# Cross-attention on one core: where SyncE's queue puts the rows of x and the tokens' values

## The chip, the core and the metric

The kernel runs on one core of a Trainium2 chip. A core has TensorE (PE: matmuls, with weight loads shown as PEld), VectorE (DVE), ScalarE (ACT), GpSimd (POOL) and SyncE (SP); each runs its own instruction stream, and they wait for one another by semaphores. Transfers between HBM and the on-chip memory are issued from SyncE's, ScalarE's or GpSimd's stream. The metric is the device time of one execution in microseconds (us).

## What is computed

`x` is 16 batches of 100 rows of 640; `ctx` is 16 batches of 722 rows of 384, of which the last 4 rows are "tokens" and the first 718 the context. There are 8 heads of 80. All is float32.

```python
query, keyt, valt = x @ Wq, enc @ Wk, enc @ Wv
hs = _mha(query, keyt, valt)                     # 100 queries over 718 keys
ca_q1 = einsum('btc,th->bch', ca, Wq_ca)[:, indices, :]
ca_hs1 = _mha(ca_q1, x, x)                       # attention over the rows of x
ca_q2 = ca_hs1 @ Wq
ca_hs2 = _mha(ca_q2, ca @ Wk_ca, ca @ Wv_ca)     # 100 queries over 4 tokens
out = (hs + ca_hs2) @ Wout + b_out + x
```

## The kernel before

A loop runs over the 16 batches `b`; the order of the instructions on each engine is the order in which the loop writes them out. In a batch PE first makes the scores (`s_ps`, L716) in three parts, with a small product `z_ps` (L934) of the token branch. VectorE takes their running maximum; the last of these maxima is called `seen` (`larger(2)`, L1380). Then PE makes values of this batch (`v_ps...`, L434, class `Values`) in turns with keys of the next (`k_ps...`, L465, class `Keys`), while VectorE and ScalarE spread the maximum, subtract it and take exponentials. At the end of the batch PE multiplies the exponentials with the values (`a_ps`, L1585: the "product with V"), makes a small product `y_ps` (L880) for a later batch, and the next batch's scores follow at once.

GpSimd does the token branch. `scores1` (L905, L912) waits for `seen`; `values2` (L1002, L1009) multiplies the values of the four tokens, spread over 100 partitions, with probabilities and adds them up. Those values lie in tiles `vb` of 250 KB: two buffers, filled for tokens 0 and 1 by `Second.load`, and for tokens 2 and 3 by SyncE out of `values2`, when the product that read the buffer before is done. `Second.load` issues its two transfers from GpSimd's stream, in the batch before the one that uses them (`second.load()`), except for batches 0 and 1. GpSimd also makes the sums `enc` (L500) that the keys and values of the next batch need, from `enc` and `rest`, which SyncE loads.

The output rows are cut into groups of 128 (`OC`); five times two of these groups are projected as a pair (`PAIRS`, `project_pair`, `o_ps` L1160, with sums on GpSimd, L1141). `Last.load` fetches the rows of `x` (`xn`, 320 KB a group) from SyncE's stream, and GpSimd adds the bias to them (L1042), so that the projection can be added on top.

SyncE's stream is worked off in order, and a transfer that waits for a semaphore holds up those behind it. In a batch it holds, in this order: rows of x where there are any, values of tokens 2 and 3, inputs of the batch after next (`xT`, `ca`, `enc`, and the small `mb`), and `rest`, which waits for PE's last key product. The rows of x stand next behind `rest` of the batch before, without a wait of their own. `wait_for(instruction, other)` makes one instruction wait for another one.

Of the kernel before, what the change touches and what calls it, by code (L numbers as in the profile page):

```python
# [126 lines left out]
def kernel(  # L127
# [18 lines left out]
    nc = tc.nc  # L146
# [131 lines left out]
    for g in range(2):  # L278
        for c in range(CC):
            nc.scalar.dma_start(  # L280
                out=wv_sb[:, 2 * c + g],
                in_=wv[c * P : (c + 1) * P, g * (H // 2) : (g + 1) * (H // 2)],
# [42 lines left out]
    for h, c, r, s, k in PIECES:  # L325
        nc.gpsimd.dma_start(
            out=m2[s : s + k, c, h - HEADS[c][0], :T],
            in_=wqcat[h * D + r : h * D + r + k, :],
# [4 lines left out]
    for c in range(HC):  # L333
        first = c * P - HEADS[c][0] * D
        nc.gpsimd.affine_select(
            out=hmask[:, c], in_=hmask[:, c], compare_op=ALU.is_ge, fill=0.0,
# [3 lines left out]
            out=hmask[:, c], in_=hmask[:, c], compare_op=ALU.is_ge, fill=0.0,  # L340
# [439 lines left out]
    def wait_for(ins, other):  # L780

        tc.add_manual_dep(
            ins.ins,
            other.ins.name,
            mybir.DependencyInfo(
                mybir.DependencyClass.Sync, mybir.DependencyReason.DATA
            ),
            reason="apart",
        )
# [69 lines left out]
    class Second:  # L859
# [87 lines left out]
            )  # L947
            self.z = z

        def load(self):  # L950
            self.vb = [self.piece(nc.gpsimd, t) for t in range(2)]

        def piece(self, engine, t):
            b = self.b
            vb = vb_tile(f"vb_{b}_{t}")
            engine.dma_start(
                out=vb[:S], in_=va_d[b * T + t].unsqueeze(0).to_broadcast([S, H])
            )
            return vb

        def scores2(self, engine=nc.vector):
# [61 lines left out]
    class Last:  # L1023
# [4 lines left out]
            self.split = b == B - 1  # L1028
            self.t_ps = None

        def load(self):

            self.xn = {}
            for r, (lo, n) in enumerate(OC):
                if self.b != O_AFTER[r]:
                    continue
                xn = self.xn[r] = spare[1] if r == len(OC) - 1 else xn_tile(f"xn_{r}")
                rows = x.rearrange("b s n -> (b s) n")[lo : lo + n]
                for at, cols in self.parts(n):
                    to = xn[at : at + n, : cols.stop - cols.start]  # L1040
                    nc.sync.dma_start(out=to, in_=rows[:, cols])
                    nc.gpsimd.tensor_tensor(to, to, bias[at : at + n, cols], ALU.add)  # L1042

        def parts(self, n):
# [201 lines left out]
    for n, heads in enumerate(HEADS):  # L1246
        cols = len(heads) * B * T
# [26 lines left out]
    second = Second(0, xT, ca_0)  # L1274
# [71 lines left out]
    for b in range(B):  # L1346
        p = b // 2
        e_in, now = enc, second
# [35 lines left out]

        if b == 0:
            enc_sums(enc)
            now.load()
            now.softmax1()
        st.append(scores(b, 0, tiles))
        if b == 0:  # L1390
# [15 lines left out]
        if b == 0:  # L1406
            second.scores1()
            m_next = load_m(b + 2)
            kk.go(3)
            top.go(3)  # L1410
            first_values(3, e_in, (act, act), get=bank)
            top.go(1)
            kk.go(2)
            now.scores2()
            now.exponentials2()
            first_values(0, e_in, (act, act), (0,), bank)
            top.go()
            kk.go(3)
            first_values(0, e_in, (act, act), (1,), bank)
            now.softmax3()  # L1420
            kk.go(2)
            subtract(0)
            exponential(0)
            kk.go(2)
            subtract(1)
            kk.go(3)
            exponential(1)
            second_next, enc_next = loads()
            less = subtract(2)
            exponential(2)  # L1430
            last_keys(b + 1, enc)
            enc_next = load_rest(b + 2, enc_next)
            keys(m_next)
            now.values2(less)
            enc_sums(enc_next)
            second.softmax1(4)
        elif b + 1 < B:
            vv = Values(b, e_in)

            def both(n):  # L1440
                vv.go(n)
                kk.go(n)

            forms = [wout_sb[:, 2 * i : 2 * i + 2, k * (H // 2) : (k + 1) * (H // 2)]
                     for i in range(2) for k in range(2)]
            if b == 2:
                for o, left, right in (
                    (forms[1], forms[1], forms[0]),
                    (wout2[:, 0], forms[3], forms[1]),
                    (wout2[:, 1], forms[2], wout2[:, 0]),  # L1450
                ):
                    nc.gpsimd.tensor_tensor(o, left, right, ALU.subtract)
            elif last.b - 1 in PAIRS:
                nc.gpsimd.tensor_tensor(wout2[:, 0], wout2[:, 0], forms[0], ALU.add)
            second.scores1(seen, range(T - 1))
            top.go(3)
            kk.go(3)
            vv.go(3)
            now.scores2(nc.gpsimd)
            second.scores1(None, range(T - 1, T))  # L1460
            if b == 1:
                now.load()
            last.load()
            top.go(1)
            if b > 1:
                last.place()
            now.exponentials2()
            both(2)
            both(2)
            top.go()  # L1470
            both(1)
            now.softmax3()
            if b == 1:
                nc.gpsimd.tensor_tensor(last.hs[:S], last.hs[:S], last.hs2, ALU.add)
            if last.b in PAIRS:
                last.sums()
            parted = b % 2 and b > 1 and last.b not in PAIRS
            now.values2(None, range(T - 1 if parted else T))
            vv.go(2)
            kk.go(1)  # L1480
            subtract(0)
            exponential(0)
            vv.go(1)
            subtract(1)
            vv.go(1)
            kk.go(2)
            exponential(1)
            vv.go(1)
            kk.go(2)
            both(1)  # L1490
            both(1)
            if b == 1:
                for f in list(wv_there):
                    nc.scalar.copy(wv_sb[:, W_AT[f]], wv_there.pop(f))
            mixed = None
            if b % 2 and b > 1:
                second_next, enc_next = loads()
                mixed = Queries(p + 1, xT_at[0], enc_next[0])
            if parted:
                mixed.sums()  # L1500
                now.values2(None, range(T - 1, T))
            else:
                second.load()
            if b == 1:
                nc.gpsimd.dma_start(out=bias, in_=bout[0].partition_broadcast(P))
            if not mixed:
                second_next, enc_next = loads()
            if b + 2 < B:
                m_next = load_m(b + 2)
            subtract(2)  # L1510
            exponential(2)
            last_keys(b + 1, enc)
            if b + 2 < B:
                enc_next = load_rest(b + 2, enc_next)
            if b == 1:
                last.transpose()
            if last.b in PAIRS:
                second.softmax1(3)
                last.project_pair()
                if last.b == max(PAIRS):  # L1520
                    nc.sync.dma_start(
                        out=forms[1],
                        in_=wout[: 2 * P, H // 2 :].rearrange("(c p) n -> p c n", p=P),
                    )
            second.softmax1(3 if parted else 8)
        else:
            room = enc_tile("spare").rearrange("p f k -> p (f k)")
            spare.extend(room[:, i * H : (i + 1) * H] for i in range(2))
            last.transpose()
            vv = Values(b, e_in)  # L1530
            last.load()
            mine.load()
            top.go(3)
            vv.go(3)
            last.project_few(len(OC) - 2)
            now.scores2(nc.gpsimd)
            now.exponentials2()
            top.go(1)
            vv.go(2)
            top.go()  # L1540
            vv.go(3)
            now.softmax3()
            now.values2()
            vv.go(2)
            subtract(0)
            exponential(0)
            vv.go(5)
            for i in (1, 2):
                subtract(i)
                exponential(i)  # L1550
            last.project()
        if b % 2 and b + 1 < B:
            xT, tiles = xT_at[0], queries_tiles(p + 1)
            if not mixed:
                for n in range(HC):
                    queries(p + 1, xT, tiles, n)
            elif parted:
                mixed.make(tiles, second.softmax1)
                second.load()
            else:  # L1560
                keys(m_next)
                mixed.sums()
                mixed.make(tiles, second.softmax1)
# [109 lines left out]
```

## Time and profile before

| | us |
|---|---|
| median of 3 runs | 922.90 |
| lowest and highest run | 922.18, 924.91 |
| profiled execution | 922.65 |
| its span, first to last instruction | 920.94 |
| PE busy in it | 911.9 |

The profile gives the busy time of each engine, who waited for whom and for how long, a timeline, the instructions and the DMA load of any stretch of time, and the chain of work that ended last. "Issue" as the releaser of a wait stands for idle time in which the engine waited for nothing that the profile shows. Times in the timeline count from the start of the span.

### The profile page before, as it was taken

The page shows a single profiled execution, that of the slowest core. Times are in us where ns is not written, and L with a number is a line of the kernel's source. Part 1 is how long each engine was busy: PE and PEld are TensorE (multiplying, and loading weights), DVE is VectorE, ACT ScalarE, POOL GpSimd, SP SyncE. Part 2 cuts the span into 40 slices and gives each one's busy share as a digit, 9 for nine tenths or more (in the row PEclk, how much of TensorE's full clock was granted, in tenths as well). Part 3 has the DMA queues.
Part 4 walks back from the last instruction along what each step waited for, and adds up shares of the span by engine and source line. Part 5 has one row for each costly group of instructions (what it writes and reads, how often), then busy time and mean ns, then how long its engine had stood idle before and what let it go on. Part 6 is the DMA issues. An engine that isn't in the chain of part 4 may idle for free.

```text
span 920.9 us, 27684 instructions
## 1 busy us (share of the span) xinstructions
PE 911.9 (99%) x11974; PEld 766.2 (83%) x11974; DVE 692.5 (75%) x1116; ACT 434.4 (47%) x836; POOL 723.6 (79%) x689
## 2 busy tenths in 40 slices
PE   9999999999999999999999999999999999999998
PEld 6988879787797979888798887988879888797966
DVE  3469895988649887795967869689784898748883
ACT  2234543737427373552737436264741737426341
POOL 5849999788977879697896969958798687976623
PEclk9999999999999999999999999999999999999999
DMA  8722013050300404031030410205030050310201
GB/s 270 269 77 78 25 49 95 1 156 2 104 32 11 119 1 134 3 97 60 24 111 3 117 40 30 77 2 155 3 101 33 2 157 1 104 46 3 81 23 38
DMA packets 49681, 62.94 MB, mean 68 GB/s; under 512 B 14072, under 2 KB 38200, under 8 KB 49560
## 3 DMA queue, kind: packets, MB, share of 16 engines
q1 hardware_dynamic: 45512, 51.49, 18.3%
q0 software_dynamic: 3024, 8.53, 3.0%
q8 instruction: 94, 1.54, 0.7%
q10 hardware_dynamic: 1024, 1.15, 0.4%
q14 instruction: 27, 0.22, 0.1%
HBM read 55.59 MB, written 5.57 MB: 66 GB/s over the span
## 4 chain that ended last, share of the span: by engine, by line
PE 97%; DVE 1%; DMA 0%; POOL 0%; issue 0%; ACT 0%; SPq 0%; ACTq 0%; POOLq 0%
PE s_ps L716 12%; PE a_ps L1585 11%; PE v_psA L434 11%; PE v_psB L434 9%; PE k_psA L465 8%; PE kT_ps L666 8%; PE k_psB L465 7%; PE o_ps L1160 5%; PE v_psC L434 4%; PE k_psC L465 3%; PE v_ps L375 2%; PE q_ps L593 2%; PE q_ps L535 2%; PE v_psD L434 2%; PE v_psE L434 2%; PE q_psA L593 1%
## 5 line engine op out<-in xcount | busy, mean ns | idle before, releaser
L905 POOL TENSOR_TENSOR e<-ca,g 100x800 f32<-100x800 f32 x64 | 99.4, 1564 | 91.8 <-ACT kT L407 64.3
L500 POOL TENSOR_TENSOR enc<-enc 128x240 f32<-128x240 f32 x135 | 106.6, 800 | 18.2 <-DMA enc<-in_enct 11.1
L1368 DVE TENSOR_TENSOR st<-st,over 120x1600 f32<-120x1600 f32 x48 | 113.8, 2373 | 0.0
L1585 PEld LDWEIGHTS a_ps<-vs,st 120*36 120x36 f32 (+3 forms) x3072 | 109.4, 124 | 3.9 <-issue 3.1
L1585 PE MATMUL a_ps<-vs,st 120*36 120x81 f32 (+3 forms) x3072 | 111.9, 233 | 0.3 <-ACT st L1376 0.3
L434 PE MATMUL v_psA<-wv_sb,enc 128*120 128x320 f32 x352 | 109.3, 433 | 0.0
L1009 POOL TENSOR_TENSOR hs<-hs,hs 100x640 f32<-100x640 f32 x48 | 96.3, 2007 | 3.8
L912 POOL TENSOR_TENSOR e<-e,e 100x800 f32<-100x800 f32 x48 | 92.1, 1919 | 3.8
L1002 POOL TENSOR_TENSOR hs<-vb,p 100x640 f32<-100x640 f32 x64 | 90.3, 1421 | 3.7 <-DMA vb<-va_d 0.9
L434 PE MATMUL v_psB<-wv_sb,enc 128*120 128x320 f32 x296 | 91.8, 433 | 0.0
L465 PE MATMUL k_psA<-enc,wk_sb 128*128 128x240 f32 x360 | 89.2, 370 | 0.0
L1376 ACT ACTIVATE st<-st 120x1600 f32<-120x1600 f32 x48 | 73.9, 1539 | 30.9 <-DVE st L1368 30.5
L434 PEld LDWEIGHTS v_psA<-wv_sb,enc 128*120 128x120 f32 x352 | 64.2, 183 | 25.0 <-DVE vs L405 0.5
L465 PEld LDWEIGHTS k_psA<-enc,wk_sb 128*128 128x128 f32 x360 | 67.2, 190 | 15.1
L1380 DVE TENSOR_TENSOR most<-most,st 120x800 f32<-120x800 f32 x64 | 67.3, 1052 | 15.5 <-ACT st L766 14.4
L716 PE MATMUL s_ps<-qp,kT 64*56 64x100 f32 (+1 forms) x3072 | 73.7, 248 | 0.6 <-issue 0.6
L465 PE MATMUL k_psB<-enc,wk_sb 128*128 128x240 f32 x300 | 73.0, 366 | 0.0
L716 PEld LDWEIGHTS s_ps<-qp,kT 64*56 64x56 f32 (+1 forms) x3072 | 67.1, 130 | 6.4 <-issue 5.2
L434 PEld LDWEIGHTS v_psB<-wv_sb,enc 128*120 128x120 f32 x296 | 54.1, 183 | 21.9 <-DVE vs L405 0.4
L1075 ACT COPY hsT<-turned_hs 32x160 f32<-32x160 f32 (+7 forms) x244 | 67.7, 278 | 3.0
L772 ACT COPY st<-s_ps 120x800 f32<-120x800 f32 x64 | 49.8, 829 | 34.3 <-PE s_ps L716 34.3
L465 PEld LDWEIGHTS k_psB<-enc,wk_sb 128*128 128x128 f32 x300 | 57.0, 190 | 7.7
(200 smaller groups left out, 1864.7 us busy)
## 6 DMA issues: line engine op xcount, KB each, us to landing
vb<-va_d POOLq DMA_DIRECT2D x32, 250.0 KB, 3.6
vb<-va_d SPq DMA_DIRECT2D x32, 250.0 KB
enc<-in_enct SPq DMA_DIRECT2D x30, 240.0 KB
enc<-in_enct SPq DMA_DIRECT2D x15, 360.0 KB
xT<-in_xt SPq DMA_DIRECT2D x8, 500.0 KB
rest<-in_enct SPq DMA_DIRECT2D x31, 120.0 KB
xn<-in_x SPq DMA_DIRECT2D x11, 320.0 KB
out<-xn SPq DMA_DIRECT2D x11, 320.0 KB
```

Source lines behind the costliest of these rows:

```text
L434: nc.tensor.matmul(at[0][j][:KN, : H // 2], a_form(self.enc, f)[:, j * KN : (j + 1) * KN], wv_there.get(f, wv_sb[:, W_AT[f]]), start=first ...
L465: nc.tensor.matmul(at[:, i * KT : (i + 1) * KT], wk_sb[:, W_AT[f], i], a_form(self.enc, f), start=(first and i == 0), stop=last, skip_grou ...
L500: nc.gpsimd.tensor_tensor(out, left, right, op)
L666: nc.tensor.matmul(bank[:, i * KT : (i + 1) * KT], weights[c], a_raw(enc, u, c), start=(i == 0 and c == 0), stop=(c == CC - 1), skip_group ...
L716: nc.tensor.matmul(s_ps[at][k0:k1, cols], w, rhs, start=not begun & {(at, k) for k in range(k0, k1, 32)}, stop=last, skip_group_check=True,)
L905: first = nc.gpsimd.tensor_tensor(to, self.ca[:, t, :].unsqueeze(1).to_broadcast([S, NH, S]), g[:, :, t].unsqueeze(2).to_broadcast([S, NH, ...
L912: nc.gpsimd.tensor_tensor(e, e, to, ALU.add)
L1002: first = nc.gpsimd.tensor_tensor(to, self.vb[t][:S].rearrange("p (h d) -> p h d", h=NH), p2[:, :, t].unsqueeze(2).to_broadcast([S, NH, D] ...
L1009: nc.gpsimd.tensor_tensor(sums, sums, to, ALU.add)
L1368: return nc.vector.tensor_tensor(st[i], st[i], top.over[:KN].unsqueeze(1).to_broadcast([KN, 2, ROWS]), ALU.subtract,)
L1376: nc.scalar.activation(st[i], st[i], AF.Exp, scale=SCALE)
L1585: nc.tensor.matmul(a_v[lo:hi, h % 4], st[i // 2][: KEYS[i], i % 2, h * S + lo : h * S + hi], block(i, h // 4)[: KEYS[i], h % 4], start=(i ...
```

## The change

`Second.load` gets an engine, SyncE unless another is named, and an instruction to wait for. It is called in the batch that uses the values, behind `seen`, and no longer in the batch before. Batch 0 keeps GpSimd. `Last.load` gets an instruction to wait for, too: between the first and the last batch the rows of x now wait for `seen`, and stand behind the values of tokens 0 and 1 in SyncE's stream. In the last batch the rows of x are issued first and wait for nothing new, and the values follow behind `seen`. No computation is changed.

```diff
-        def load(self):
-            self.vb = [self.piece(nc.gpsimd, t) for t in range(2)]
-
-        def piece(self, engine, t):
+        def load(self, engine=nc.sync, behind=None):
+            self.vb = [self.piece(engine, t, behind) for t in range(2)]
+
+        def piece(self, engine, t, behind=None):
             b = self.b
             vb = vb_tile(f"vb_{b}_{t}")
-            engine.dma_start(
+            dma = engine.dma_start(
                 out=vb[:S], in_=va_d[b * T + t].unsqueeze(0).to_broadcast([S, H])
             )
+            if behind:
+                wait_for(dma, behind)
             return vb
...
-        def load(self):
+        def load(self, behind=None):
...
-                    nc.sync.dma_start(out=to, in_=rows[:, cols])
+                    dma = nc.sync.dma_start(out=to, in_=rows[:, cols])
+                    if behind:
+                        wait_for(dma, behind)
                     nc.gpsimd.tensor_tensor(to, to, bias[at : at + n, cols], ALU.add)
...
         if b == 0:
             enc_sums(enc)
-            now.load()
+            now.load(nc.gpsimd)
             now.softmax1()
...
             second.scores1(None, range(T - 1, T))
-            if b == 1:
-                now.load()
-            last.load()
+            now.load(behind=seen)
+            last.load(seen)
             top.go(1)
...
             if parted:
                 mixed.sums()
                 now.values2(None, range(T - 1, T))
-            else:
-                second.load()
...
             last.load()
             mine.load()
+            now.load(behind=seen)
             top.go(3)
...
             elif parted:
                 mixed.make(tiles, second.softmax1)
-                second.load()
             else:
```

## The prediction

> **What bounds the kernel now.** I read the page first: which engine is full, and what the chain that ended last is made of.
>
> ```profile
> span 920.9 us, 27684 instructions
> ...
> PE   911.9 (99%) x11974; PEld 766.2 (83%) x11974; DVE 692.5 (75%) x1116; ACT 434.4 (47%) x836; POOL 723.6 (79%) x689
> ...
> q8 instruction: 94, 1.54, 0.7%
> ...
> vb<-va_d POOLq DMA_DIRECT2D x32, 250.0 KB, 3.6
> ...
> rest<-in_enct SPq DMA_DIRECT2D x31, 120.0 KB
> xn<-in_x SPq DMA_DIRECT2D x11, 320.0 KB
> ```
>
> TensorE is busy for all but 9 us. The edit takes no matmul away, so it can give back only time in which PE stood still. Next come the waits of PE alone, then the timeline at the places where it stood still inside the loop over batches; the bracket holds the idle time before the row.
>
> ```profile
> PE z_ps L934 <- issue: 1.1, 3, 0.6
> PE y_ps L880 <- POOL enc L500: 0.8, 1, 0.8
> ...
> PE s_ps L716 <- issue: 0.6, 2, 0.5
> ```
>
> ```profile
> 204.38 1.25 PE L716 MATMUL s_ps<-qp,kT 64*56 64x100 f32 x46 [0.47 <-issue]
> ...
> 211.95 0.45 PE L934 MATMUL z_ps<-y_sb,e 100*32 100x33 f32 x31 [0.58 <-issue]
> ...
> 644.73 0.52 PE L880 MATMUL y_ps<-m,xT 128*64 128x108 f32 x8 [0.77 <-POOL enc L500]
> ...
> 758.02 1.17 PE L716 MATMUL s_ps<-qp,kT 64*64 64x100 f32 x44 [0.17 <-issue]
> ...
> 830.74 0.26 PE L934 MATMUL z_ps<-y_sb,e 100*32 100x33 f32 x6 [0.22 <-issue]
> ...
> 877.85 0.25 PE L934 MATMUL z_ps<-y_sb,e 100*32 100x33 f32 x5 [0.28 <-issue]
> ```
>
> Six stops, 0.47 + 0.58 + 0.77 + 0.17 + 0.22 + 0.28 = 2.49 us. Five of them have "issue" as releaser: PE waited for nothing that the profile shows. What they have in common shows when the instructions between them are counted:
>
> ```profile
> 204.37:211.94 7.57, 6.99 (x255) 6.17 (x255) 3.43 (x4) 4.12 (x8) 6.99 (x8) 1.00 0.02 4
> 211.94:644.72 432.78, 432.01 (x5715) 364.75 (x5714) 336.22 (x546) 217.61 (x426) 353.09 (x333) 1.00 0.20 60
> 644.72:758.01 113.29, 113.12 (x1524) 95.17 (x1524) 87.59 (x140) 56.46 (x112) 92.04 (x88) 1.00 0.20 60
> 758.01:830.73 72.72, 72.50 (x1144) 61.03 (x1144) 51.02 (x81) 34.35 (x69) 59.68 (x59) 1.00 0.15 48
> 830.73:877.84 47.11, 46.83 (x635) 39.41 (x635) 41.08 (x63) 25.32 (x49) 32.03 (x22) 1.00 0.13 41
> ```
>
> The first two counts of each row are PE's matmuls and weight loads. Together: 510, 11429, 3048, 2288, 1270. Whole multiples of 256 are 512, 11520, 3072, 2304, 1280; every count is under its multiple by less than 1%, and semaphore instructions, which also stand in PE's stream, are not in these counts. So all six stops lie a whole number of 256 instructions apart. The queue named "instruction" moved 94 packets of 1.54 MB / 94 = 16.4 KB, and PE has 2 x 11974 = 23948 instructions: 23948 / 94 = 255 per packet. My reading: PE's instructions come in blocks of 256 by DMA, and each stop is a block that was not there in time. That covers the stop at 644.73 too, which the view puts down to GpSimd.
>
> **Why a block is late.** DMA share and GB/s (last two columns) around three of the stops, and around a product with V that no stop follows:
>
> ```profile
> 196.00:201.70 5.70, 5.70 (x168) 5.70 (x165) 5.37 (x12) 1.31 (x3) 2.63 (x8) 1.00 0.90 243
> 201.85:203.90 2.05, 2.05 (x57) 1.78 (x53) 1.63 (x6) 0.00 (x0) 1.97 (x4) 1.00 0.02 6
> 637.20:642.25 5.05, 5.05 (x150) 5.05 (x147) 4.84 (x10) 0.71 (x3) 2.79 (x7) 1.00 0.85 276
> 642.35:643.90 1.55, 1.55 (x46) 1.46 (x41) 1.25 (x3) 0.33 (x1) 1.55 (x2) 1.00 0.01 3
> 750.20:755.60 5.40, 5.40 (x159) 5.40 (x156) 5.15 (x11) 1.07 (x3) 3.00 (x9) 1.00 0.82 261
> 309.40:314.80 5.40, 5.40 (x155) 5.40 (x155) 5.15 (x13) 0.98 (x3) 3.35 (x8) 1.00 0.59 157
> ```
>
> In the three bad stages the queues are at 0.82 to 0.90 until 201.70, 642.25 and 755.60 and then empty; PE goes on at 204.38, 644.73 and 758.02, that is 2.7, 2.5 and 2.4 us after they emptied. A nearly constant distance from the end of the loads is what a block that waits behind them would show. What those loads are, for the middle one:
>
> ```profile
> 635.93 1.10 POOL L956 DMA_DIRECT2D vb<-va_d  x2
> ...
> 636.64 0.82 SPq L232 DMA_DIRECT2D rest<-in_enct  x2
> 637.51 0.90 SPq L1041 DMA_DIRECT2D xn<-in_x  x2
> ```
>
> In bytes: rest 2 x 120 KB, the tokens' values (vb) 2 x 250 KB, rows of x (xn) 2 x 320 KB, together 1380 KB; the change takes the last two kinds, 1140 KB of them, out of this stage. The stage at 309.40 has rest and vb alone, at 157 GB/s, and no stop. PE runs 150 + 147 instructions in 5.05 us there, so a block of 256 lasts 4.4 us, and 5 us of loads are just enough to use it up.
>
> **The change part by part.** (1) Out of the product with V. Left is rest: 240 KB at 276 GB/s, 0.9 us in place of 5.1. The loads then end some 4 us earlier, against stops of 0.47, 0.77 and 0.17 us, so all three go. The 0.58 us at 211.95 lies exactly two blocks after the one at 204.38, in the same scores, where a block lasts 7.57 / 2 = 3.8 us and a late one has no time to be caught up; I take it as the same delay and let it go too. Gain 0.47 + 0.58 + 0.77 + 0.17 = 1.99 us. The stops at 830.74 and 877.85 come at the end of scores ahead of which hardly anything was loaded; for the first:
>
> ```profile
> 822.93:830.50 7.57, 7.57 (x302) 6.73 (x298) 4.75 (x7) 4.15 (x8) 1.18 (x1) 1.00 0.02 5
> ```
>
> Share 0.02, and 600 instructions in 7.57 us, so that a block lasts 3.2 us: there PE outruns its blocks by itself, and I leave both stops. Bounds: 0 if the stops have another cause, 2.49 us if all six go.
>
> (2) Into the stretch behind the scores. `seen` is the last maximum of the scores; SP now waits for it before the values of tokens 0 and 1 and, in five batches, before the rows of x behind them. What needs them:
>
> ```profile
> 721.00 1.54 POOL L905 TENSOR_TENSOR e<-ca,g 100x800 f32<-100x800 f32 x1 [9.73 <-ACT kT L407]
> ...
> 736.21 2.50 POOL L1002 TENSOR_TENSOR hs<-vb,p 100x640 f32<-100x640 f32 x2
> ...
> 766.96 2.01 DVE L1380 TENSOR_TENSOR most<-most,st 120x800 f32<-120x800 f32 x2
> ...
> 781.40 3.05 POOL L1042 TENSOR_TENSOR xn<-xn,bias 128x640 f32<-128x640 f32 x2
> ```
>
> GpSimd waits for the same `seen` before L905, so the first use of vb is 736.21 - 721.00 = 15.2 us behind it. In a batch with rows of x, `seen` ends at 766.96 + 2.01 = 768.97 and the bias is added at 781.40, 12.4 us later. Price of the loads: SP already issues such a pair of vb, for tokens 2 and 3:
>
> ```profile
> 737.51 1.53 SPq L956 DMA_DIRECT2D vb<-va_d  x2
> ...
> 738.20:741.90 3.70, 3.70 (x19) 3.19 (x18) 3.70 (x4) 1.97 (x2) 3.54 (x3) 1.00 0.57 157
> ```
>
> At 157 GB/s 500 KB take 3.2 us; from the issue to the end of that window are 741.90 - 737.51 = 4.4 us. The rows of x at the same rate take another 640 / 157 = 4.1 us, so all is there by some 8.5 us, with 3.9 us left for the bias and 10.8 us for vb. Cost on the path: nothing; without that cover each microsecond of lateness would fall on GpSimd. Bounds: 0, and what the slower rival below gives. The wait itself holds up in SP's queue only the rows of x and the values of tokens 2 and 3, and the latter wait for GpSimd's first products at 736.21 anyway; rest, the stores and the next batch's inputs stand ahead of the waiting load or behind those.
>
> (3) GpSimd no longer issues 30 of its 32 loads of vb, 1.10 us a pair by the row at 635.93: 16.5 us in all. It stands 9.73 us idle at `seen`, so this only lengthens that idle time: 0. SP takes 1.53 us a pair instead, and has nothing else to do there.
>
> (4) The last batch: its values now come behind `seen`, the rows of x keep their place ahead of them.
>
> ```profile
> 878.74 2.01 DVE L1380 TENSOR_TENSOR most<-most,st 120x800 f32<-120x800 f32 x2
> ...
> 893.97 2.51 POOL L1002 TENSOR_TENSOR hs<-vb,p 100x640 f32<-100x640 f32 x2
> ```
>
> `seen` ends at 880.75, the use is 13.2 us later, the load needs 4.4: 0.
>
> Sum, against the profiled execution (922.65 us, of which the span is 920.94): 922.65 - 1.99 = 920.66. That execution lies 0.25 us under the median of 922.90, so it stands for an ordinary run.
>
> **The rivals.** *The stops stay* (922.65 us). They would be something that happens to fall on 256 and not code behind loads; or the block read in advance reaches further than I think. For it: the stop at 830.74 follows no loads. Against it: the 2.4 to 2.7 us, and the stage at 309.40, which has fewer bytes and no stop. The Trainium skill, "Runtime: NRT & Kernel Launch", section "Instruction fetch mechanics", says that PE holds 2048 instructions, refilled in blocks of 256; by it PE would have 1792 instructions in hand and loads of 5 us could not stop it, which gives this rival's 922.65 us. The same section also speaks of two blocks only, and the counts above fit that. Chance 0.10.
>
> *Part of it* (921.3 to 922): one or two of the four stops remain, because rest, still in that stage, delays a block enough, or because the stop at 211.95 is like the two late ones. With the 0.58 staying, 922.65 - 1.41 = 921.24. Chance 0.13.
>
> *All of it* (922.65 - 2.49 = 920.16 us): blocks that come earlier also take away the late two. Chance 0.12.
>
> *Slower*: the rows of x come too late for the bias, and GpSimd is late with the pair's sums, on which PE's output product waits.
>
> ```profile
> 787.00 2.25 POOL L1141 TENSOR_TENSOR hsT<-sum,hsT 128x256 f32<-128x256 f32 x1
> ...
> 797.78 9.69 PE o_ps L1160 x36
> ```
>
> The sums end at 789.25, PE needs them at 797.78: 8.5 us of room. So it decides only when the rows land over 12.4 + 8.5 = 20.9 us behind `seen`, in place of my 8.5; each microsecond beyond costs 1 us in each of five batches. 2 us beyond would give 920.66 + 10 = 930.7. For it: the loads now follow one another in one queue. Against: that needs 1140 KB at 55 GB/s, while the slowest row above has 157. Chance 0.06.
>
> **How the numbers follow.** The forecast case has the remaining 0.59. Range: the low end is 920.16 less the 0.72 by which the fastest run of before lies under its median (922.18), 919.4; the high end is the case in which nothing goes, at 922.65, and half a microsecond for the spread of a median, 923.2. Left out is the slower rival. About 0.3%, or 2.77 us, can be told from no change; 920.13 is the limit from the median. The forecast misses it by half a microsecond, and a run of before went to 924.91, so the kernel may well have more such stops than this execution shows: I give the forecast case two in five for faster, the full case two in three, 0.24 + 0.08, and 0.02 for spread, 0.34. Slower is the last rival and spread, 0.07. Same is the rest, 0.59.
>
> **What would show it.** In the profile after: no PE idle at the scores whose products with V ran beside xn (204, 644 and 758 us here), the instruction counts between any stops that remain still multiples of 256; DMA share of those stages near 0.2, and a burst behind each `seen` instead; GpSimd without a wait for DMA before L1042's and L1002's successors; GpSimd's busy time unchanged and its loads two. Wrong would be stops at the same three places, new ones behind `seen`, or a bias that waits for its rows.

## The result and the profile after

| | before | after |
|---|---|---|
| median, 8 runs each (us) | 923.37 | 919.07 |
| lowest and highest run | 922.18, 926.58 | 918.38, 921.99 |
| profiled execution | 922.65 | 919.14 |
| its span | 920.94 | 917.40 |

The ratio is 0.9952, with a 95% interval of 0.9937 to 0.9968: faster by about 0.5%, 4.3 us by the medians. The forecast was 920.7; the result lies 0.3 us under the range, and "faster by over 0.3%" had been given 0.34.

The page of the kernel after: engine, busy time, share of the span, instructions; then the queue of instruction blocks and the loads of the values.

```profile
span 917.4 us, 27706 instructions
...
PE 910.1 (99%) x11974; PEld 765.7 (83%) x11974; DVE 692.3 (75%) x1116; ACT 434.3 (47%) x836; POOL 706.2 (77%) x659
...
q8 instruction: 94, 1.54, 0.7%
...
vb<-va_d SPq DMA_DIRECT2D x62, 250.0 KB
```

PE's instructions and its 94 blocks are the same. GpSimd has 30 instructions less, all of them issues, and SyncE now issues 62 of the 64 loads of values. The prediction's signs had GpSimd's busy time unchanged; it fell by 17.4 us (723.6 to 706.2), because these issues count in it (16.5 us by the prediction's step (3)). The waits of PE after (what waited for what: us in total, times, longest):

```profile
PE idle_ps L1230 <- DVE idle L1227: 1.1, 1, 1.1
PE y_ps L880 <- POOL m L852: 0.7, 1, 0.7
PE z_ps L934 <- issue: 0.6, 2, 0.3
PE v_ps L375 <- DMA wv_sb<-in_wv: 0.6, 1, 0.6
PE m_ps L1265 <- issue: 0.5, 1, 0.5
```

The waits "PE s_ps L716 <- issue" and "PE y_ps L880 <- POOL enc L500" are gone. The timeline of PE after, at the scores that had the first stop, and at the only two stops inside the loop:

```profile
201.41 0.93 PE L880 MATMUL y_ps<-m,xT 128*36 128x72 f32 x20
202.27 1.60 PE L716 MATMUL s_ps<-qp,kT 64*64 64x100 f32 x64
203.80 1.63 PE L716 MATMUL s_ps<-qz,kT 32*120 32x200 f32 x32
...
322.32 0.32 PE L934 MATMUL z_ps<-y_sb,e 100*32 100x33 f32 x15 [0.29 <-issue]
...
827.79 0.26 PE L934 MATMUL z_ps<-y_sb,e 100*32 100x33 f32 x6 [0.32 <-issue]
```

The 64 matmuls of the first scores stand in one row without a bracket; before, they broke off at 204.38. The stop at 827.79 is the one that stood at 830.74; the one at 322.32 is new, before has no bracket at that place. The windows of the kernel after, over the three products with V, over the stretch between these two stops, and behind the scores of batch 13 (last two columns: DMA share and GB/s):

```profile
194.90:200.70 5.80, 5.80 (x170) 5.80 (x167) 5.50 (x12) 1.23 (x3) 4.96 (x10) 1.00 0.17 47
322.31:827.78 505.47, 505.11 (x6859) 426.37 (x6858) 388.44 (x626) 252.23 (x496) 402.24 (x373) 1.00 0.20 59
634.90:640.00 5.10, 5.10 (x151) 5.10 (x148) 4.89 (x11) 0.70 (x2) 4.30 (x9) 1.00 0.20 54
747.40:752.80 5.40, 5.40 (x159) 5.40 (x157) 5.16 (x12) 0.84 (x3) 4.57 (x9) 1.00 0.19 51
766.00:772.50 6.50, 6.50 (x28) 4.85 (x27) 6.01 (x14) 5.58 (x12) 6.26 (x5) 1.00 0.71 180
```

The three products have a DMA share of 0.17 to 0.20 in place of 0.90, 0.85 and 0.82, and the burst is in the last row. Between the two stops lie 6859 + 6858 = 13717 matmuls and weight loads, 0.8% under 54 x 256 = 13824: these stops, too, fall on ends of blocks. The moved loads and their users in the timeline after, batches 12, 13 and 15:

```profile
718.15 3.04 POOL L905 TENSOR_TENSOR e<-ca,g 100x800 f32<-100x800 f32 x2 [9.72 <-DVE most L1384]
733.53 2.50 POOL L1004 TENSOR_TENSOR hs<-vb,p 100x640 f32<-100x640 f32 x2
...
763.43 2.01 DVE L1384 TENSOR_TENSOR most<-most,st 120x800 f32<-120x800 f32 x2
765.50 0.71 SPq L956 DMA_DIRECT2D vb<-va_d  x2
766.26 0.83 SPq L1043 DMA_DIRECT2D xn<-in_x  x2
777.86 4.65 POOL L1046 TENSOR_TENSOR xn<-xn,bias 128x640 f32<-128x640 f32 x2
...
877.76 0.70 SPq L956 DMA_DIRECT2D vb<-va_d  x2
890.68 2.50 POOL L1004 TENSOR_TENSOR hs<-vb,p 100x640 f32<-100x640 f32 x2
```

`seen` ends at 765.44, the issue follows at once, the burst is over by about 772.5, and the bias is added at 777.86, 12.4 us behind `seen`, without a bracket that names a DMA. What GpSimd waits for values at all, over the whole kernel after, is one row of its waits (0.9 us in three waits before):

```profile
POOL hs L1004 <- DMA vb<-va_d: 1.0, 4, 0.3
```

Where the time of the profiled pair went, from PE's start of the first scores of a batch to that of the next (in batch 15 to the start of PE's last matmul), in us:

| | to the scores of batch 0 | batch 0 | batch 1 | batches 2 to 14 | batch 15 | rest | span |
|---|---|---|---|---|---|---|---|
| before | 59.62 | 39.03 | 57.17 | 714.16 | 46.60 | 4.36 | 920.94 |
| after | 59.90 | 38.55 | 56.27 | 712.32 | 46.26 | 4.11 | 917.40 |
| difference | +0.28 | -0.48 | -0.90 | -1.84 | -0.34 | -0.25 | -3.54 |

### The profile page after: what moved, and what is told of

Its sections match the earlier page's. It is cut to its first block, busy times and chain, and to the rows that moved or that the text cites. A ratio compares the mean times of both kernels' runs of the same rounds, so it can differ in the third digit from the quotient of the medians.

```text
span 917.4 us, 27706 instructions
## 1 busy us (share of the span) xinstructions
PE 910.1 (99%) x11974; PEld 765.7 (83%) x11974; DVE 692.3 (75%) x1116; ACT 434.3 (47%) x836; POOL 706.2 (77%) x659
## 4 chain that ended last, share of the span: by engine, by line
PE 99%; DMA 0%; issue 0%; DVE 0%; POOL 0%; ACTq 0%; POOLq 0%
PE s_ps L716 12%; PE a_ps L1586 12%; PE v_psA L434 11%; PE v_psB L434 9%; PE k_psA L465 8%; PE kT_ps L666 8%; PE k_psB L465 7%; PE o_ps L1164 5%; PE v_psC L434 4%; PE k_psC L465 3%; PE v_ps L375 2%; PE q_ps L593 2%; PE q_ps L535 2%; PE v_psD L434 2%; PE v_psE L434 2%; PE q_psA L593 1%
## 5 line engine op out<-in xcount | busy, mean ns | idle before, releaser
L500 POOL TENSOR_TENSOR enc<-enc 128x240 f32<-128x240 f32 x135 | 109.0, 817 | 18.3 <-DMA enc<-in_enct 11.1
L1372 DVE TENSOR_TENSOR st<-st,over 120x1600 f32<-120x1600 f32 x48 | 113.3, 2362 | 0.0
L1384 DVE TENSOR_TENSOR most<-most,st 120x800 f32<-120x800 f32 x64 | 65.0, 1015 | 15.4 <-ACT st L766 14.2
L716 PE MATMUL s_ps<-qp,kT 64*56 64x100 f32 (+1 forms) x3072 | 73.1, 248 | 0.0
L716 PEld LDWEIGHTS s_ps<-qp,kT 64*56 64x56 f32 (+1 forms) x3072 | 66.9, 130 | 5.4 <-issue 4.2
```

The lines of the kernel that those rows point to most:

```text
L500: nc.gpsimd.tensor_tensor(out, left, right, op)
L716: nc.tensor.matmul(s_ps[at][k0:k1, cols], w, rhs, start=not begun & {(at, k) for k in range(k0, k1, 32)}, stop=last, skip_group_check=True,)
L1372: return nc.vector.tensor_tensor(st[i], st[i], top.over[:KN].unsqueeze(1).to_broadcast([KN, 2, ROWS]), ALU.subtract,)
```

## The experiments

Theory A is the prediction's: instruction blocks of PE stand behind the bytes of a burst of loads. Its rivals were that GpSimd's issue beside the product with V does the harm (B), and that the difference is spread between runs. Ratios are against the kernel before, run on the same chip in the same session.

**One half of the change at a time.** Values behind `seen`, rows of x where they were (`e1_values_only`, edit against the kernel after):

```diff
+            last.load()
             now.load(behind=seen)
-            last.load(seen)
```

> Only the values of tokens 0 and 1 move (SyncE, behind the scores); the rows of x stay beside the product with V, without a wait. Theory A (PE's instruction blocks queue behind the loads beside the product with V): the three stages keep rest and rows of x, 880 KB, about 3.3 us of loads in place of 5.1; a block lasts 4.4 us there, so the stops at the scores of batches 3, 11 and 13 should go, and the time should be 3 to 4.3 us under the kernel before. Rival B (the gain is GpSimd's, which issues 30 loads less): the whole 4.3 us. A shows in the stops, B in GpSimd alone.

Rows of x behind `seen`, values from GpSimd as before (`e2_rows_only`, edit against the kernel before, with the new argument of `Last.load`):

```diff
-            last.load()
+            last.load(seen)
```

> Only the rows of x move behind the scores; the values of tokens 0 and 1 are issued by GpSimd in the batch before, as before. Theory A: the three stages keep rest and values, 740 KB in about 4.8 us, like the stage at 309 us of before which no stop followed; the stops should go or shrink, 2 to 4.3 us under the kernel before. Rival B (GpSimd's issue is what costs): no gain, within 0.5 us of before.

Measured: 921.38 us for e1, ratio 0.9965 (0.9951 to 0.9979); 919.72 for e2, ratio 0.9961 (0.9944 to 0.9977). By the ratios that is 3.2 and 3.6 us under the kernel before, by the medians of the session 3.4 and 5.0. In neither profile does PE stop at the three places. So each half alone takes the stops away, and the two gains don't add up: rest and rows of x (880 KB) are not enough for a stop there, rest and values (740 KB) neither, all three (1380 KB) can be. e2 leaves GpSimd's issue where it was and has no stops, which speaks against B for these stops. The profile of e1 has 41.15 us for batch 0; that comes back below.

**The place without the queue.** Values behind `seen`, but issued by GpSimd (`e3_gpsimd_behind`, against the kernel after):

```diff
-            now.load(behind=seen)
+            now.load(nc.gpsimd)
             last.load(seen)
```

> Both kinds of load behind the scores as in the change, but the values are still issued by GpSimd, in the batch that uses them. Theory A: only the place counts, so the time is that of the change, 4 us under before, within 0.7 us. Rival B (GpSimd's issue): the time of before, within 0.7 us.

Measured: 924.07 us, ratio 1.0004 (0.9990 to 1.0018). The three stops are gone, and yet nothing is gained. One row of PE's waits and the timeline of batch 3 in e3 say why:

```profile
PE k_psC L465 <- DVE vs L405: 2.8, 5, 0.6
```

```profile
225.66 1.09 POOL L956 DMA_DIRECT2D vb<-va_d  x2
226.72 4.79 DVE L1372 TENSOR_TENSOR st<-st,over 120x1600 f32<-120x1600 f32 x1
226.77 3.05 POOL L1046 TENSOR_TENSOR xn<-xn,bias 128x640 f32<-128x640 f32 x2
...
231.96 1.08 PE L465 MATMUL k_psC<-enc,wk_sb 128*128 128x240 f32 x4 [0.56 <-DVE vs L405]
```

The same two instructions in the timeline of the kernel after:

```profile
225.38 3.05 POOL L1046 TENSOR_TENSOR xn<-xn,bias 128x640 f32<-128x640 f32 x2
...
226.43 3.68 DVE L1372 TENSOR_TENSOR st<-st,over 120x1600 f32<-120x1600 f32 x1
```

GpSimd's issue of 1.09 us now stands right ahead of the bias addition, which so starts 1.4 us later, at 226.77, and lies wholly beside VectorE's subtraction L1372: that takes 4.79 in place of 3.68 us, VectorE comes 1 us later to the values it has to take out of PE's way, and PE stands for 0.56. That happens in the five batches with rows of x. Batches 2 to 14 take 716.50 us, 4.2 more than in the kernel after. Theory A had the stops right and the time wrong, since it counted GpSimd's issue at nothing in any place. Rival B's number, the time of before, came true, but through this wait behind the scores and not through the product with V.

**The kernel before once more** (`e4_before_again`, no edit):

> The kernel before once more, for a second profile of it. Theory A: PE stops again at the scores of batches 3, 11 and 13 (near 204, 645 and 758 us), a whole number of 256 instructions apart, perhaps at further places; the ratio is 1.000 within 0.002. Rival C (the stops of one execution are chance): other places and counts that are no multiples.

Measured: 922.27 us against 924.75 for the same kernel in the same session, ratio 0.9981 (0.9968 to 0.9994): two sets of runs of one kernel can be 0.2% apart, so an interval here is somewhat too narrow. Its profile has one large stop, again ahead of batch 11, and only small ones in batches 3 (0.29, at the second place of before) and 13 (0.16 and 0.39); one of 0.39 in batch 2 and the second one in batch 13 stand where before has none. The large one in the waits of PE:

```profile
PE y_ps L880 <- POOL enc L500: 1.1, 1, 1.1
```

So the stops behind the bursts come back in the same batches and all stops lie at ends of blocks, but neither their length nor the small ones are the same in each execution.

**Shifting the ends of the blocks.** 32 small matmuls on zeros ahead of the loop, recorded as 64 matmuls and 64 weight loads: half a block more. Once in the kernel after (`e5_after_half_block`), once in the kernel before (`e6_before_half_block`):

```diff
+    for _ in range(32):
+        nc.tensor.matmul(idle_ps[:32, :32], idle[:, :32], idle[:, :32], start=True, stop=True)
```

> The changed kernel with 32 small matmuls on zeros in front of PE's work (128 more instructions, half a block; they add up to 2.5 us at the start and nothing to the result). Theory A: block ends lie half a block elsewhere; the loads beside the product with V are too short to matter, so no stops of half a microsecond or more at the scores of batches 3, 11, 13, and the time from the first scores to the end stays within 1 us of the change's. Rival C (chance): the same.

> The kernel before with the same 128 instructions in front. Theory A: a block that was asked for at 199 us and needed at 203.9 us is now asked for near 197 and needed near 201.5, but still comes only when the loads have drained at 201.7 and 2.4 to 2.7 us after that: the three stops move 128 instructions and grow to 1.5 to 3 us each, so from the first scores to the end this is 2 to 7 us longer than before. Rivals B and C: no longer than before by more than 1 us.

Measured: e5 922.08 us, ratio 1.0001 (0.9991 to 1.0012); e6 923.58, ratio 1.0012 (1.0000 to 1.0023). Both times say little, since the additional matmuls also make the start some 1 us longer and batch 0 slower (40.7 and 40.8 us). In batches 2 to 14, e5 takes 711.17 us without any of the stops and e6 713.32 with one of them (0.69 us, PE goes on at 204.66) and a new one of 0.41 at 382.25. The longer time expected of e6 did not come; a reading that fits is that a burst costs something only where PE asks for its next block at certain points of it. In e6 the transfer of the late block began at 202.18, with loads under way until after 203, so "it waits until the queues are empty" was too simple.

**More bytes beside the product with V.** First with a gap: rows of x loaded twice more there, each second load of a tile waiting for the first (`e7_useless_loads`, against the kernel after; the real loads stay behind `seen`):

```diff
+            if behind:
+                for r, (lo, n) in enumerate(OC):
+                    if self.b == O_AFTER[r]:
+                        self.xn[r] = xn_tile(f"xn_{r}")
+                        for _ in range(2):
+                            nc.sync.dma_start(
+                                out=self.xn[r][:n],
+                                in_=x.rearrange("b s n -> (b s) n")[lo : lo + n],
+                            )
...
```

> The change, and beside the product with V the rows of x loaded twice more into their own tiles, from SyncE, without a wait (1280 KB that nobody reads); the real loads stay behind the scores. GpSimd issues as few loads as in the change. Theory A: stops at the scores of batches 3, 11 and 13 are back, 0.4 to 1 us each by the places where PE goes on, and the time is 1.5 to 3.5 us over the change's. Rival B: the change's time within 0.7 us.

Measured: 918.91 us, ratio 0.9970 (0.9959 to 0.9981), by its median as quick as the kernel after, which was not run in that session, and no stop at the three places (batches 2 to 14: 711.47 us). Theory A's number was missed, and rival B's met. The windows of e7 around the product of batch 3:

```profile
198.00:200.60 2.60, 2.60 (x80) 2.60 (x77) 2.49 (x6) 0.14 (x1) 2.35 (x7) 1.00 0.76 217
200.60:202.30 1.70, 1.70 (x55) 1.70 (x52) 1.67 (x2) 0.00 (x0) 1.62 (x3) 1.00 0.06 16
202.30:205.00 2.70, 2.70 (x78) 2.62 (x78) 2.40 (x7) 0.87 (x1) 2.54 (x4) 1.00 0.76 243
```

The loads came as two bursts of some 2.6 us with 1.7 us of empty queues between them, and the block of this stage came through in that gap: its transfer began at 200.87. So the next kernel loads the same bytes as before, at the same place, without a gap (`e13_useless_like_before`, against the kernel after): in even batches values and rows of x once more, right behind `rest`, all from SyncE; the real loads, into the same tiles, stay behind `seen`.

```diff
+            if b % 2 == 0:
+                second.load_early()
+                mine.load_early()
             second.softmax1(3 if parted else 8)
```

> The change, and in every even batch the values and the rows of x loaded once more where they stood in before, right behind rest, but all from SyncE and without a gap between them (1380 KB with rest); the loads that count stay behind the scores. If bytes in one burst make PE's block late, whoever issues them: the stops at the scores of batches 3, 11 and 13 are back, batches 2 to 14 take 1 to 2.5 us more than the change's 712.3. If it takes loads from GpSimd's own queue beside SyncE's: no such stops, 711.3 to 712.6.

Measured: 923.33 us, ratio 0.9995 (0.9980 to 1.0010), against 0.9959 (0.9945 to 0.9973) for the kernel after in the same session. The stops are back in batches 3 and 13, here in the timeline of PE:

```profile
204.22 1.25 PE L716 MATMUL s_ps<-qp,kT 64*56 64x100 f32 x46 [0.75 <-issue]
...
211.79 0.45 PE L934 MATMUL z_ps<-y_sb,e 100*32 100x33 f32 x31 [0.58 <-issue]
...
758.90 1.43 PE L716 MATMUL s_ps<-qp,kT 64*64 64x100 f32 x56 [1.24 <-issue]
```

and the windows of e13, over the product with V ahead of the first stop and from the second to the third:

```profile
196.20:201.75 5.55, 5.55 (x164) 5.55 (x161) 5.28 (x9) 0.87 (x1) 5.41 (x10) 1.00 0.89 236
211.79:758.89 547.10, 545.48 (x7239) 460.19 (x7238) 428.39 (x687) 274.23 (x539) 436.19 (x403) 1.00 0.22 67
```

The burst is that of before (0.89 at 236 GB/s), the first two stops lie within 0.2 us of their places before, and 14477 instructions are 0.8% under 57 x 256 = 14592. Batches 2 to 14 take 715.63 us, 3.3 more than in the kernel after (1 to 2.5 had been expected). No engine computes with these loads, and GpSimd issues none of them: this shows that a burst of loads alone stops PE. The Trainium skill, "Runtime: NRT & Kernel Launch", section "Instruction fetch mechanics", gives PE a store of 2048 instructions; by that, 5.5 us of loads could not have stopped it, and the measured 1.24 us decide against it. The two blocks of 256 that the same section speaks of agree with these rows. Batch 11 did not stop in e13; the next paragraph has the reason.

**The blocks on their way.** The traces hold the 94 transfers of the queue "instruction" one by one, and a narrow window shows where one begins: 546 GB/s over 0.03 us are 16.4 KB. A transfer counts in the window in which it begins, with its whole length, so a share of 2.15 is 2.15 x 16 x 0.03 = 1.03 us. The blocks of the three stages, in before (in its second and third window some other transfers begin, too):

```profile
201.77:201.80 0.03, 0.03 (x8) 0.03 (x4) 0.03 (x1) 0.00 (x0) 0.03 (x1) 1.00 2.15 546
642.30:642.34 0.04, 0.04 (x8) 0.04 (x5) 0.03 (x1) 0.04 (x1) 0.00 (x0) 1.00 1.90 538
755.69:755.72 0.03, 0.03 (x8) 0.03 (x5) 0.03 (x1) 0.03 (x1) 0.03 (x1) 1.00 2.22 632
```

and in after:

```profile
198.54:198.57 0.03, 0.03 (x8) 0.03 (x5) 0.03 (x1) 0.00 (x0) 0.03 (x1) 1.00 2.62 546
637.67:637.70 0.03, 0.03 (x8) 0.03 (x5) 0.03 (x1) 0.00 (x0) 0.03 (x2) 1.00 2.17 546
750.43:750.46 0.03, 0.03 (x7) 0.03 (x4) 0.03 (x1) 0.00 (x0) 0.03 (x1) 1.00 1.97 546
```

How late is that? If PE's semaphore instructions are counted too, the six stops of before lie whole multiples of 256 apart to within one instruction, so each end of a block can be found in the trace. From PE's passing of one end to the start of the next block's transfer, in us, and whether PE stopped at the end that followed:

| | batch 3 | batch 11 | batch 13 |
|---|---|---|---|
| before | 2.6, stop | 3.1, stop | 2.6, stop |
| e4 (before again) | 1.8, none | 3.4, stop | 2.6, stop |
| e12 (before, ordered batch 0) | 3.0, stop | 3.4, stop | 3.0, stop |
| e13 (useless loads) | 3.1, stop | 2.0, none | 3.6, stop |
| e1 (rest and rows of x) | 0.7, none | 1.9, none | 1.2, none |
| e2 (rest and values) | 0.2, none | 1.3, none | 0.7, none |
| after (rest alone) | 0.2, none | 0.3, none | 0.0, none |

In the 14 profiles PE has 37 stops of 0.15 us or more from 110 us on that are put down to "issue" or, like the one at 644.73, to GpSimd's sums; in all of them PE goes on 1.3 to 1.6 us after the end of a block's transfer, and that transfer took 0.9 to 1.5 us. So a block that lasts 4.4 us leaves room for a start some 4.4 - 1.0 - 1.4 = 2.0 us late, and the table turns from none to stop just there. This shows the mechanism itself: the burst delays the block, and the late block stops PE. It also clears GpSimd of the stop at 644.73: in e12 the same row starts at 644.83, while the nearest of GpSimd's sums end at 644.15 and 645.04. And the second stop of batch 3 is the first one's delay handed on: its block began 1.4 us behind the end of the one before it, in after 0.5.

**Batch 0.** Left over was the part ahead of batch 2. Values of batch 0 from SyncE instead of GpSimd (`e10_batch0_synce`, against the kernel after):

```diff
-            now.load(nc.gpsimd)
+            now.load()
```

> The change, with the values of batch 0 issued by SyncE too. In batch 0 an execution of the values-only kernel stood 2.6 us longer, in code that all these kernels share: VectorE's second maximum took 4.96 us beside GpSimd's issue of the two loads and its first product, against 2.38 in the change's profile. If that race is with the issue, the runs lose their slow group near 922 us and the median is at or under the change's, 918 to 919; if it is with the product that follows, nothing changes.

Measured: 920.63 us, ratio 0.9985 (0.9974 to 0.9997): no gain. A new stop of 1.22 us, with "issue" as releaser, stands at batch 0's `z_ps` (PE goes on at 68.98), and batch 0 takes 39.97 us. But batch 0 also differs between executions of one kernel. Its maxima and GpSimd's first product in the timeline of the kernel after (batch 0 takes 38.55 us):

```profile
69.39 2.38 DVE L1384 TENSOR_TENSOR most<-most,st 120x800 f32<-120x800 f32 x2
72.03 3.05 POOL L905 TENSOR_TENSOR e<-ca,g 100x800 f32<-100x800 f32 x2
```

and in that of e1 (41.15 us):

```profile
70.10 4.96 DVE L1384 TENSOR_TENSOR most<-most,st 120x800 f32<-120x800 f32 x2
71.16 3.04 POOL L905 TENSOR_TENSOR e<-ca,g 100x800 f32<-100x800 f32 x2
```

In batch 0 GpSimd's `scores1` does not wait for `seen`. Where its first product runs beside VectorE's second maximum (in e1 it starts 0.05 us behind it), the two maxima take 4.96 us in place of 2.38, and PE later waits 1.6 us for keys. The same edit in both kernels, after (`e11_after_ordered`) and before (`e12_before_ordered`), orders them:

```diff
         if b == 0:
-            second.scores1()
+            second.scores1(seen)
```

> The change, and in batch 0 GpSimd's first token product waits for the last maximum of the scores, as it does in every later batch. Theory A now has two parts: the stops at block ends, worth about 2 us of the batches from 2 on, and a race in batch 0, in code that before and change share, in which GpSimd's first product slips in ahead of VectorE's last maximum and the batch takes up to 2.6 us more. With the wait batch 0 takes 38.6 us in every execution; the runs have no slow group, median 918 to 919.

> The kernel before with that same wait in batch 0. Two-part theory: 1.8 to 2.6 us slower than the change with the wait, which is then the worth of the change itself, and 0 to 2 us faster than the kernel before. Rival (the whole 4 us measured belong to the moved loads): still 4 us slower than the change with the wait.

Measured in one session: e11 919.44 us (917.87 to 920.00), ratio 0.9947 (0.9931 to 0.9963); e12 922.50 (921.32 to 923.85), ratio 0.9986 (0.9975 to 0.9997). Batch 0 takes 38.55 us in both profiles. The difference of the change with that race out of the way is 922.50 - 919.44 = 3.06 us (3.6 by the two ratios), and no run of the one lies within the runs of the other. A gain of 1.8 to 2.6 had been expected, or 4 by the rival: it is neither; and e11's median had been expected at 918 to 919. PE's waits in e12 are those of before:

```profile
PE y_ps L880 <- POOL enc L500: 1.2, 1, 1.2
PE s_ps L716 <- issue: 1.2, 2, 0.7
...
PE z_ps L934 <- issue: 0.9, 3, 0.3
```

**The kernel after once more** (`e14_after_again`, no edit), in the session of e11 to e13:

> The change once more, beside the two with the ordered batch 0: batches 2 to 14 take 711.3 to 712.6 us again with no stop at the scores of batches 3, 11 and 13; its runs fall in two groups, near 918.6 and 1 to 3 us above.

Measured: 920.92 us (918.24 to 922.21), ratio 0.9959 (0.9945 to 0.9973), 3.15 us under the 924.07 of the kernel before in that session. Three runs lie at 918.2 to 919.3, the other six at 920.1 to 922.2; the profiled one (920.14) has no stops in batches 2 to 14 (711.13 us), and 38.95 and 57.75 us for batches 0 and 1. The kernel e11 has the lowest median of its session, 1.5 us under this one, but the two intervals overlap.

## Why the prediction was right or wrong

**The mechanism: right.** The stops at 204.38, 211.95, 644.73 and 758.02 went with the loads, e13 brings stops back with bytes that nobody uses, and the transfers of the blocks show the delay itself: up to 3.6 us behind such a burst, 0.3 at most beside rest alone. The constant 2.4 to 2.7 us of the prediction are the block's own transfer, 1.0 us, and the 1.4 to 1.6 until PE goes on. The rivals in which the stops stay, or some of these four, are out. Whether all six go depends on the execution: the small late stops come and go, two of 0.3 us in after, none behind batch 1 in e14. At 322.32 the block's transfer took 1.38 us; in before, which has no stop there, 0.96.

**The sum: the term (1), 1.99 us, was too small; this is the step that failed.** It was added up from brackets. If the starts of the same PE instructions are set side by side in the two traces, the four stops are worth 0.71 + 0.77 + 0.95 + 0.35 = 2.78 us, about 0.2 more for each. The bracket opens at the modelled end of the matmul before. A single one of these is drawn about 0.25 us long, while 64 of them take 1.60 us together in the row at 202.27, some 20 ns each from start to start; so the bracket leaves out the first 0.2 us of a stop. That the batches 2 to 14 of this pair differ by 1.84 us, close to the 1.99, is luck: at five other ends of blocks, 322.32 among them, PE stood 0.13 to 0.47 us longer in after than in before, 1.1 us in all. And one execution was too few: batches 2 to 14 take 714.16, 714.61 and 715.59 us in three profiles with the old order (before, e4, e12), and 712.32, 711.13 and 712.36 in three with the new one (after, e14, e11), means 714.79 and 711.94. That is 2.85 us; the ordered pair gives 3.06 by its medians, the unordered one in that session 3.15; by the ratios these two are 3.6 and 3.8. The change is worth about 3 us, 0.33%, not the 4.3 of the first medians.

**The rest of the 4.3 us is not from the moved loads, as far as the runs show.** In the profiled pair 0.48 + 0.90 = 1.38 us of the gain stand in batches 0 and 1. There, one and the same kernel differs by as much: 94.82 us in the profile of after and 96.70 in that of e14, 96.20 in that of before and 94.82 in that of e4. It is not the race of e1 that does it here: the two maxima take 2.4 us in all four, but GpSimd's first product starts at 73.35 in before and 73.78 in e14, at 72.03 and 72.21 in the quick two; why, was not found. With batch 0 ordered the median of after is 1.5 us lower and that of before 1.6, which is within the 0.2% that two sets of one kernel can differ by. The first set of runs of after was mostly quick, seven of eight under 919.6, against three of nine in e14; why the shares differ was not found.

**The range failed with it.** Its low end came from the profiled execution of before, taken as an ordinary one; three of its four stops are shorter than those of e12 or e13 at the same places. The remark that other executions may have more of them was right and was given too little weight: it went into the chance of "faster" and not into the time.

**Steps (2) and (4), cover: right.** The bias comes 12.4 us behind `seen`, as forecast, with the burst over some 7 us behind it (8.5 forecast); values are used 15.4 us behind `seen` in batch 12 and 12.9 us behind the issue in the last. GpSimd's waits for values are 1.0 us in all, 0.9 before. So the slower rival, with a bias that waits for its rows, is out by more than 13 us.

**Step (3), GpSimd's issues: nothing where they stood, as forecast, but not nothing in every place.** e2 keeps them at the product with V and loses nothing that shows. e3 puts them ahead of the bias addition, and the same 1.1 us cost 4 us in five batches.

**"The block waits until the loads have drained": wrong in this form.** In before the three transfers begin within 0.1 us of the end of the loads; e6 and e7 show blocks that came during the loads or in a gap. What the table has: beside the product with V, one unbroken burst of 1380 KB delayed the block by 1.8 to 3.6 us, 880 or 740 KB (e1, e2) by up to 1.9, and PE stood still where it was more than 2.0. So what a burst costs, from nothing to 1.24 us, differs from place to place and from execution to execution. Which of the loads a block has to wait for was not measured; that it hangs on where in the burst PE asks for it is argued from e6 and e7, not shown.

## What to carry to other kernels

When a nearly full PE waits for "issue", count the matmuls and weight loads between such waits: whole multiples of 256 point to late instruction blocks, and then to the loads of the 5 us ahead of each. The transfers of the queue "instruction" show directly when each block was on its way. Break a long burst up or move part of it to a stretch where a block lasts longer; here either half was enough, though the rows of x alone left little room (1.9 us late ahead of batch 11, against some 2.0). Size such a stop by the starts of the same instructions in two traces and over several executions, not by one bracket.

## What the runs showed of the hardware that was not expected

A load that no engine computes with stops PE by up to 1.24 us (e13), and PE still stands 2 us after the queues have emptied: ahead of the stop below the block's transfer ran from 201.77 to 202.87, and PE went on 1.35 us after its end. The windows of e13 ahead of the stop that ends at 204.22:

```profile
201.00:201.75 0.75, 0.75 (x28) 0.75 (x25) 0.65 (x2) 0.44 (x1) 0.69 (x2) 1.00 0.94 335
201.75:202.20 0.45, 0.45 (x19) 0.45 (x16) 0.36 (x2) 0.00 (x0) 0.43 (x1) 1.00 0.64 219
202.20:204.20 2.00, 1.28 (x34) 1.00 (x31) 1.93 (x5) 0.36 (x1) 1.92 (x3) 1.00 0.02 9
```

An instruction of GpSimd's queue can cost VectorE as much as its own time: 1.09 us of issue, set ahead of a bias addition, made a subtraction 1.11 us longer (4.79 against 3.68). The issue itself does not do it: in e11 it lies beside the two maxima of batch 0 (69.69 to 70.85), and they take 2.01 us. It is the instruction behind it: the two maxima of batch 0 took 4.96 in place of 2.38 us beside GpSimd's product. The Trainium skill, "SBUF — State Buffer", section "Who interferes with whom", says that a VectorE instruction with two inputs in this memory contends with a GpSimd instruction that reads it; the 2.58 us of batch 0 and the 1.11 us of e3 agree with it. In both it is VectorE's instruction that takes longer, although the trace has it start 0.05 us ahead of GpSimd's.
